# Graph attention over sorted edges: query rows fetched per tile of 128 edges, with one product in place of three

## The chip, the cores and the metric

The kernel runs on one core of a Trainium2 chip. The metric is the device time of one execution in microseconds. The engines are named as in the profile: PE (TensorE, matrix products), PEld (its weight loads), DVE (VectorE), ACT (ScalarE), POOL (GpSimd) and SP (SyncE, which here only starts DMAs and reads the addresses for them).

## The reference

One layer of relational graph attention with a residual and two layer norms. There are 3125 nodes with 128 features, 100,000 edges sorted by destination, 5 edge types (relations) and 8 heads of 16 features. For each relation `r`:

```
q = einsum('eh,khd->ekd', x[dst], W_Q[r]); k, v = the same with x[src], W_K[r], W_V[r]
logits = (q * k).sum(-1) / 4 + attn_bias[r]            # only edges of type r
exp_l  = exp(logits - segment_max(logits, dst)[dst])
attn   = exp_l / (segment_sum(exp_l, dst)[dst] + 1e-12)
out   += segment_sum(attn[:, :, None] * v, dst)
```

Then `out @ out_proj_w.T + out_proj_b`, the residual `x` and a layer norm, the residual again and a second layer norm. An edge needs the query row of its destination and type, and the key and value rows of its source and type.

## The kernel before

**Head.** Nodes come in 25 blocks of 128. For each block the key and value rows of every node and relation are computed (`table`) and stored to DRAM in `kv_d`, one row of 256 float32 for each pair of node and relation. The query rows of a block are split into three bf16 parts whose sum is the float32 row (the value, the remainder, and the remainder of that) and stored in `q_d`, 3 x 128 bf16 for each pair of node and relation; the head does so for the first four blocks. Other jobs prepare, for each edge, the index of its source row, a key that tells its destination and type apart within its group, masks, and `first5`, the row of `q_d` at which a group's window begins. Some sums test that the destinations are sorted and dense enough; if not, a general path runs, which is not executed here.

**Main loop.** Edges come in groups of 512, a group is 4 tiles of 128 edges, and a step has 3 groups, thus 12 tiles (the last two steps have 2 groups). There are 66 steps. Schedule and order are written by hand: each engine runs its instructions in the order of the program, so the order of the calls in the loop (L1003 to L1075) is the order of work. Step k holds work of several steps:

- `gather(k+3)` (L603, POOL): 12 indirect DMAs, one for each tile, bring the key and value rows of 128 edges into one of 6 buffers. Step k+3 takes the buffer that `weigh` has emptied (L817).
- `queries` (L622, PE), for the block due: 3 relations in one step, 2 in the next. The three parts are made by ACT (L627, L636) and DVE (L631, L640).
- `exped(k-2)`: 8 passes on PE bring the exponentials back to the edges (`ex`, L802), ACT copies them (L811). `lanes_turned(k-1)` turns logits (L752), ACT copies (L771).
- `products(k)` (L702, DVE): key rows times the query rows `qe`.
- `spread_q(k+1, [0, 1])` (L688, PE), and later in the step `spread_q(k+1, [2])`: the query row of each edge. `hot` says for each edge which of the 125 rows of the group's window (25 nodes by 5 relations) is its own; the products of `hot` with the three parts add up in PSUM. That is 3 products for each tile, 36 in a step: 24 behind `products`, 12 ahead of the second `sums`.
- `norm(k-3)` (L857 to L861, DVE), the third query part (L640, DVE) and, when a block's rows are complete, `store_q` (L644, SP). Then `relations(k-3)` (`nodes`, L874, PE) and `by_node` (L879, ACT), for which ACT reads a group's first node into a register (L589), one read for each group.
- `weigh(k-2)` (L817, DVE): value rows times exponentials, then `sums` (L845, L841, PE), three times in a step, over the matrices that `places` (L825, L828, ACT) makes.
- `logits(k)` (L722, L711, L728, DVE), `pass_on` (L743, ACT), `turn_next(k-1)` (L752, PE), `spot(k+2)` (`hot`, L675, DVE), `shares(k-1)`: scans (L777, L780) and L787 on DVE, the exponential on ACT (L795).
- `take(k)` on SP: `fetch(k+3)` loads the keys broadcast to 128 partitions (`kt`, L653) and, for each group, reads the row number (L589) and loads 128 rows of 768 bytes (`qw`, L660); then the masks of step k+1 (L667) and, where due, the store of a result block (L945). `kt` has 2 buffers, `qw` 3, `hot` 2.

The blocks that are done are projected, added and normed between (L886 to L937). The lines at which the change touches the loop:

```
products(k)
spread_q(k + 1, [0, 1])
...
third_part(q, c0)
if c0:
    store_q(q)
...
spread_q(k + 1, [2])
if k + 2 < NST:
    spot(k + 2)
...
take(k)
```

Of the kernel before, what the change touches and what calls it, by code (L numbers as in the profile page):

```python
# [50 lines left out]
WR = WN * R  # L51
RH = 3
LANES = R * HEADS
L3 = G3 * LANES
# [70 lines left out]
def windowed_path(  # L125
# [22 lines left out]
    first = keep("first", [1, NGR], I32)  # L148
    first5 = keep("first5", [1, NGR], I32)
    oT = keep("oT", [P, N + WN])  # L150
# [23 lines left out]
    nc.vector.memset(xn[:, NT - 1, :], 0.0)  # L174
    fr = load.tile([1, NGR], I32, name="fr")
    wn = load.tile([2 * R * HEADS, H * HD], F32, name="wn")
# [12 lines left out]
    with nc.allow_non_contiguous_dma(reason="one element of each group"):  # L189
        nc.sync.dma_start(  # L190
            fr[:, : NGR - 1], dst[: (NGR - 1) * GE].rearrange("(o g i) -> o g i", o=1, i=GE)[:, :, 0]
        )
        nc.sync.dma_start(
            fr[:, NGR - 1 : NGR],
            dst[(NGR - 1) * GE : (NGR - 1) * GE + 1].rearrange("(o g) -> o g", o=1),
        )
# [70 lines left out]
    nc.vector.memset(ones, 1.0)  # L267
    vio = keep("vio", [P, 6])
    nc.vector.memset(vio, 0.0)
# [64 lines left out]

    def spills():
# [9 lines left out]
        )  # L345

    gather_heads = keep("gather_heads", [P, G3, HEADS])
# [30 lines left out]
    kvrow = load.tile([HG, 2, GE], F32, name="kvrow")  # L378
    keyr = load.tile([HG, 2, GE], F32, name="keyr")
    typr = load.tile([HG, 2, GE], F32, name="typr")  # L380

    def keys_a():
# [85 lines left out]
    def sorted_ends():  # L468
# [14 lines left out]
        nc.vector.tensor_reduce(vio[0:1, 5:6], lrf[:, 1, :], AX.X, ALU.add)  # L483

    def checks():
        vp = pps.tile([P, 6], F32, name="vp", tag="tr", bufs=2)
        nc.tensor.matmul(vp, ones, vio, start=True, stop=True)
        nc.vector.tensor_reduce(vio[:, 0:1], vp, AX.X, ALU.add)
        nc.vector.tensor_scalar_add(n_bad_i, vio[0:1, 0:1], -float(PADS))

# [40 lines left out]


    first_q = 4
    tps, xts, prs = [], [], []
    for b in range(first_q):
# [5 lines left out]
        for c0, c1 in ((0, RH), (RH, R)):  # L541
# [11 lines left out]
            )  # L553
        nc.sync.dma_start(
            q_d[b * P * R : (b + 1) * P * R, :].rearrange("(p r) c -> p (r c)", r=R),
            q3.rearrange("p r s h -> p (r s h)"),
        )

    sorted_rows()
    short_rows()  # L560
    sorted_ends()
    checks()
    nc.scalar.dma_start(beta_t, beta.partition_broadcast(P))
# [23 lines left out]

    def window(g, table, engine):
        return nc.values_load(  # L589
            table[0:1, g : g + 1],  # L590
            engines=[engine],
            min_val=0,
            max_val=(N - 1) * (R if table is first5 else 1),
            skip_runtime_bounds_check_because="destinations are nodes",
        )

    SPE, ACTE = mybir.EngineType.SP, mybir.EngineType.Activation
# [44 lines left out]
    def store_q(b):  # L642
        live.pop(("xT", b))
        nc.sync.dma_start(  # L644
            q_d[b * P * R : (b + 1) * P * R, :].rearrange("(p r) c -> p (r c)", r=R),
            live.pop(("q3", b)).rearrange("p r s h -> p (r s h)"),
        )

    def fetch(k):
        gs = groups(k)  # L650
        n = len(gs)
        kt = flow.tile([P, G3, GE], BF16, name="kt", bufs=2)
        nc.sync.dma_start(  # L653
            kt[:, :n].rearrange("w g e -> w (g e)"),
            key_d[gs[0] : gs[0] + n].rearrange("g e -> (g e)").partition_broadcast(P),
        )
        qw = flow.tile([P, G3, 3, H], BF16, name="qw", bufs=3)
        for i, g in enumerate(gs):
            f = window(g, first5, SPE)
            nc.sync.dma_start(qw[:, i].rearrange("w s h -> w (s h)"), q_d[bass.ds(f, P), :])  # L660
        live["kt", k], live["qw", k] = kt, qw
# [10 lines left out]
    def spot(k):  # L672
        n = len(groups(k))
        hot = flow.tile([WR, G3, GE], BF16, name="hot", bufs=2)
        nc.vector.tensor_scalar(  # L675
            hot[:, :n], live.pop(("kt", k))[:WR, :n], row_of[:WR], None, op0=ALU.is_equal
        )
        live["hot", k] = hot

    def spread_q(k, which=range(G3)):  # L680
        hot, qw, n = live["hot", k], live["qw", k], len(groups(k))
        if which[0] == 0:
            live["qe", k] = ps.tile([P, T * G3, H], F32, name="qe")
        qe = live["qe", k]
        for i in which:
            for t in range(T if i < n else 0):
                for s in range(3):
                    nc.tensor.matmul(  # L688
                        qe[:, t * n + i, :], hot[:, i, t * P : (t + 1) * P], qw[:WR, i, s, :],
                        start=(s == 0), stop=(s == 2),  # L690
                    )
        if which[-1] == G3 - 1:
            del live["hot", k], live["qw", k]

# [306 lines left out]
    for k in range(NST - 1):  # L1001
# [28 lines left out]
        products(k)  # L1030
        spread_q(k + 1, [0, 1])
        if q is not None:
# [21 lines left out]
        if new:  # L1054
            turn_next(k - 1)
        spread_q(k + 1, [2])
        if k + 2 < NST:
# [583 lines left out]
```

## Time and profile before

| | us |
|---|---|
| median of the runs (3) | 1592.48 |
| lowest and highest | 1590.37 and 1599.27 |
| the profiled execution | 1604.74 |
| its span, first to last instruction | 1602.9 |

| engine | busy us | share of the span |
|---|---|---|
| PE | 1026.0 | 64% |
| PEld | 776.9 | 48% |
| DVE | 887.8 | 55% |
| POOL | 765.3 | 48% |
| ACT | 637.9 | 40% |

The granted clock of PE is 0.689 on average. The first gather starts at 79.9 us and the last at about 1508; in between lie the steps of the main loop, most of them 20 to 24 us long. The DMA engines moved 193.33 MB in 99,495 packets, 18,923 of them under 512 bytes. A line of the table of groups reads: source line, engine, operation, output and inputs, count, then busy us and mean ns of one, then the engine's idle time ahead of it and what ended most of it. "remote" and "another core or an unknown queue" there stand for a wait whose releaser the profile could not name. A line of a timeline reads: start, us, engine, line, operation, output and inputs, count, and in brackets the idle time ahead.

### The profile page before, as it was taken

How to read it: one execution, taken by the hardware profiler on the slowest of the kernel's cores; microseconds unless marked ns; L12 is line 12 of the kernel's file. 1: busy time of each engine (PE TensorE's matmuls, PEld its weight loads, DVE VectorE, ACT ScalarE, POOL GpSimd, SP SyncE). 2: the span in 40 equal slices, each digit the busy share in tenths (PEclk: the TensorE clock that was granted, in tenths of full speed). 3: DMA queues.
4: the chain of work that ended last, by engine and by line, in shares of the span. 5: the costliest groups of instructions: out<-in, count | busy, mean ns of one | idle time of the engine just before them, and what ended most of it. 6: DMA issues, size and time to landing. Idle time of an engine off the chain costs nothing.

```text
span 1602.9 us, 18517 instructions
## 1 busy us (share of the span) xinstructions
PE 1026.0 (64%) x6087; PEld 776.9 (48%) x6087; DVE 887.8 (55%) x1288; ACT 637.9 (40%) x1700; POOL 765.3 (48%) x850
## 2 busy tenths in 40 slices
PE   8930367766657656766657665666556756667985
PEld 4420345544546544554445554455444544455764
DVE  5630455655546555655556655565645655555873
ACT  3410134443434434443434443444434444444662
POOL 2077255555454555455455555555545545455300
PEclk9955667676576677666677666777677766676766
DMA  7655243453443343453444343353344343444300
GB/s 245 265 179 143 87 134 97 123 144 103 119 133 102 106 124 101 118 147 105 117 133 115 101 130 104 110 155 111 106 123 132 97 136 105 120 136 121 80 7 8
DMA packets 99495, 193.33 MB, mean 121 GB/s; under 512 B 18923, under 2 KB 58878, under 8 KB 99270
## 3 DMA queue, kind: packets, MB, share of 16 engines
q0 software_dynamic: 37728, 102.55, 23.9%
q1 hardware_dynamic: 60530, 88.20, 18.0%
q10 hardware_dynamic: 1132, 1.31, 0.3%
q8 instruction: 50, 0.82, 0.2%
q14 instruction: 55, 0.45, 0.1%
HBM read 161.59 MB, written 30.40 MB: 120 GB/s over the span
## 4 chain that ended last, share of the span: by engine, by line
another core or an unknown queue 26%; DVE 26%; PE 22%; ACT 13%; issue 9%; DMA 2%; POOL 1%; DVEq 0%; ACTq 0%
PE both L845 7%; DVE lt L780 4%; DVE lt L777 4%; ACT at L825 4%; PE pr L366 3%; DVE wv L817 3%; PE nodes L874 3%; PE qe L688 3%; DVE lg L722 3%; DVE prod L702 2%; ACT at L828 2%; DMA floor<-in_L_gnn_attn_bias 2%; PE both L841 2%; ACT ls L795 1%
## 5 line engine op out<-in xcount | busy, mean ns | idle before, releaser
L603 POOL DMA_INDIRECT kv<-kv_d,idx x782 | 755.2, 966 | 740.3 <-DVE wv L817 452.6
L688 PE MATMUL qe<-qw,hot 125*128 125x128 bf16 x2352 | 263.3, 277 | 323.9 <-issue 224.4
L688 PEld LDWEIGHTS <-hot 125*128 125x128 bf16 x2352 | 204.0, 127 | 363.9 <-issue 270.5
L845 PE MATMUL both<-wv,at 128*125 128x136 f32 x1568 | 366.3, 375 | 17.6 <-ACT oT L879 10.8
L845 PEld LDWEIGHTS both<-wv,at 128*125 128x125 f32 x1568 | 283.5, 251 | 90.0 <-issue 63.8
L825 ACT ACTIVATE at<-row_at,nkey 128x125 f32<-128x125 f32 x784 | 247.4, 388 | 0.8
L631 DVE TENSOR_TENSOR prq<-prq,q 128x384 f32<-128x384 f32 (+1 forms) x42 | 21.0, 500 | 320.0 <-ACT q L627 320.0
L874 PE MATMUL nodes<-rsum,o 125*128 125x25 f32 x392 | 91.9, 378 | 142.9 <-DVE q L640 136.1
L874 PEld LDWEIGHTS nodes<-rsum,o 125*128 125x128 f32 x392 | 85.6, 315 | 158.2 <-DVE q L640 149.8
L702 DVE TENSOR_TENSOR prod<-kv,qe 128x1536 f32<-128x1536 f32 (+1 forms) x66 | 114.5, 1735 | 65.1 <-remote 59.3
L811 ACT COPY wv<-ex 128x96 f32<-128x96 f32 (+1 forms) x66 | 15.6, 236 | 311.6 <-remote 286.5
L828 ACT ACTIVATE at<-at 128x500 f32<-128x500 f32 x196 | 121.5, 620 | 6.2
L817 DVE TENSOR_TENSOR wv<-kv,ex 128x1536 f32<-128x1536 f32 (+1 forms) x66 | 114.1, 1728 | 10.5 <-ACT wv L811 10.5
L777 DVE TENSOR_TENSOR_SCAN lt<-mk,lt 120x640 f32<-120x640 bf16 (+1 forms) x66 | 98.6, 1493 | 34.5 <-issue 19.7
L722 DVE TENSOR_REDUCE lg<-prod 128x96 f32<-128x1536 f32 (+1 forms) x66 | 115.2, 1745 | 2.3
L780 DVE TENSOR_TENSOR_SCAN lt<-mk,lt 120x640 f32<-120x640 bf16 (+1 forms) x66 | 98.7, 1495 | 2.3
L906 DVE TENSOR_TENSOR h<-pj,xn 128x128 f32<-128x128 f32 (+1 forms) x25 | 7.3, 291 | 158.1 <-remote 140.4
L841 PE MATMUL both<-wv,over 128*5 128x136 f32 x390 | 94.8, 333 | 0.0
L795 ACT ACTIVATE ls<-ls 120x512 f32<-120x512 f32 (+1 forms) x66 | 41.6, 630 | 127.0 <-DVE ls L787 49.2
L752 PE MATMUL lt<-ident,lx 128*120 128x128 f32 (+2 forms) x396 | 84.0, 309 | 4.8 <-DVE lx L711 2.0
L802 PEld LDWEIGHTS ex<-gather_heads,ls 120*128 120x128 f32 (+1 forms) x528 | 75.3, 213 | 20.4 <-issue 10.3
L743 ACT COPY lx<-lx 64x40 f32<-64x40 f32 x65 | 14.4, 222 | 162.5 <-DVE lx L728 153.1
(150 smaller groups left out, 971.4 us busy)
## 6 DMA issues: line engine op xcount, KB each, us to landing
kt<-key_d SPq DMA_DIRECT2D x64, 384.0 KB
qw<-q_d SPq DMA_DIRECT2D x196, 96.0 KB
kv_d<-kvs SPq DMA_DIRECT2D x24, 640.0 KB
kv<-kv_d,idx POOLq DMA_INDIRECT x782
q_d<-q SPq DMA_DIRECT2D x25, 480.0 KB
mk<-msk_d SPq DMA_DIRECT2D x64, 150.2 KB
out<-z SPq DMA_DIRECT2D x24, 64.0 KB
xn<-in_x SPq DMA_DIRECT2D x2, 448.0 KB
```

The costliest lines, as they stand in the source:

```text
L603: nc.gpsimd.indirect_dma_start(out=kv[:, t * n + i, :], out_offset=None, in_=kv_d[:, :], in_offset=bass.IndirectOffsetOnAxis(ap=idx[:, t, ...
L688: nc.tensor.matmul(qe[:, t * n + i, :], hot[:, i, t * P : (t + 1) * P], qw[:WR, i, s, :], start=(s == 0), stop=(s == 2),)
L702: nc.vector.tensor_tensor(prod[:, :n], kv[:, :n, :H], qe[:, :n], op=ALU.mult)
L722: nc.vector.tensor_reduce(lg, heads(live.pop(("prod", k))[:, : T * n]), AX.X, ALU.add)
L777: nc.vector.tensor_tensor_scan(lt, mk[:n, :WIDE], lt, -BIG, op0=ALU.add, op1=ALU.max)
L780: nc.vector.tensor_tensor_scan(lt[:, ::-1], mk[:n, WIDE:0:-1], lt[:, ::-1], -BIG, op0=ALU.add, op1=ALU.max)
L817: nc.vector.tensor_tensor(heads(wv[:, :n, :H]), heads(kv[:, :n, H:]), ex[:, :, :, None].to_broadcast([P, n, HEADS, HD]), op=ALU.mult,)
L825: nc.scalar.activation(at[:, t, :], row_at[:, :WR], AF.Abs, bias=nkey[:, t, g : g + 1], scale=1.0)
L828: nc.scalar.activation(at, at, AF.Relu, bias=1.0, scale=-1.0)
L841: nc.tensor.matmul(pp[:R], over[:, g, :], live["wv", last][:, t * len(groups(last)) + j, :], start=False, stop=False,)
L845: nc.tensor.matmul(pp[:WR], at[:, t, :], wv[:, t * n + i, :], start=(t == 0), stop=(t == T - 1))
L874: nc.tensor.matmul(nodes[:, i], o5[:, i], rsum[:WR], start=True, stop=True)
```

## The change

Each tile of 128 edges gets a window of its own: 8 nodes by 5 relations are 40 rows of 3 parts. In `q_d` each part is now a row of its own (256 bytes), so that a window is 120 rows that follow each other. `qw` holds the 120 rows of each of the 12 tiles, one load for each tile: 12 loads of 120 x 256 bytes in a step in place of 3 loads of 128 x 768. `hot` has 120 partitions, three for each pair of node and relation, and the three parts add up inside one product: 12 products in a step in place of 36, all of them behind `products`. The keys count from the first node of the tile instead of the group; `row_in` is a partition's number divided by 3. The row numbers of a group's four tiles are read together, by one register load on SP for each group; ACT reads the three first nodes of a step in one. `store_q` is moved behind `take`, thus behind the fetches of the step on SP. In the head the first destination of each tile is loaded (781 elements in place of 195, plus the last), and two more sums test that no tile spans more than 8 nodes.

Over the whole run the instructions of `qe` fall from 2352 to 784 on PE; on SP the loads of `qw` rise from 196 to 784.

```diff
+QN = 8
+QR = QN * R
+NTILE = -(-E // P)
...
-    q_d = dram.tile([NP * R, 3 * H], BF16, name="q_d")
+    q_d = dram.tile([NP * R * 3, H], BF16, name="q_d")
...
         nc.sync.dma_start(
-            fr[:, : NGR - 1], dst[: (NGR - 1) * GE].rearrange("(o g i) -> o g i", o=1, i=GE)[:, :, 0]
+            fr[:, : NTILE - 1],
+            dst[: (NTILE - 1) * P].rearrange("(o g i) -> o g i", o=1, i=P)[:, :, 0],
         )
...
-        nc.vector.tensor_copy(frf, fr)
-        nc.vector.tensor_copy(first, frf)
-        nc.vector.tensor_scalar_mul(first5, frf, float(R))
+        nc.vector.tensor_copy(frf, fr[:, ::T])
+        nc.vector.tensor_copy(first, fr[:, ::T])
+        nc.vector.tensor_scalar_mul(first15, fr, float(R * 3))
...
     def lanes():
+        third = load.tile([P, 2], I32, name="third")
+        nc.vector.tensor_scalar_mul(third[:, 0:1], row_of, 171.0)
+        nc.vector.tensor_scalar(
+            third[:, 1:2], third[:, 0:1], 9, None, op0=ALU.arith_shift_right
+        )
+        nc.vector.tensor_copy(row_in, third[:, 1:2])
...
+        nc.vector.tensor_copy(near, keyr[:, :, ::P])
...
-        nc.vector.tensor_copy(keyb, keyr)
+        nc.vector.tensor_tensor(
+            keyb.rearrange("g s (t i) -> g (s t) i", i=P),
+            keyr.rearrange("g s (t i) -> g (s t) i", i=P),
+            near.rearrange("g s t -> g (s t)")[:, :, None].to_broadcast([HG, 2 * T, P]),
+            op=ALU.subtract,
+        )
...
+    def short_tiles():
+        spans = load.tile([HG, 2, T], F32, name="spans")
+        nc.vector.tensor_tensor(
+            spans, dst_r[:, :, P - 1 :: P], dst_r[:, :, ::P], op=ALU.subtract
+        )
...
+    def store_rows(b, q3):
+        nc.sync.dma_start(
+            q_d[b * P * R * 3 : (b + 1) * P * R * 3, :].rearrange("(p c) h -> p (c h)", c=3 * R),
+            q3.rearrange("p r s h -> p (r s h)"),
+        )
...
-    def window(g, table, engine):
-        return nc.values_load(
-            table[0:1, g : g + 1],
+    def starts(table, a, b, engine):
+        _, at = nc.values_load_multi_w_load_instructions(
+            table[0:1, a:b],
             engines=[engine],
...
     def fetch(k):
...
-        kt = flow.tile([P, G3, GE], BF16, name="kt", bufs=2)
+        kt = flow.tile([3 * QR, G3, GE], BF16, name="kt", bufs=2)
...
-        qw = flow.tile([P, G3, 3, H], BF16, name="qw", bufs=3)
+        qw = flow.tile([3 * QR, T * G3, H], BF16, name="qw", bufs=3)
         for i, g in enumerate(gs):
-            f = window(g, first5, SPE)
-            nc.sync.dma_start(qw[:, i].rearrange("w s h -> w (s h)"), q_d[bass.ds(f, P), :])
+            for t, f in enumerate(starts(first15, g * T, (g + 1) * T, SPE)):
+                nc.sync.dma_start(qw[:, t * n + i, :], q_d[bass.ds(f, 3 * QR), :])
...
-        hot = flow.tile([WR, G3, GE], BF16, name="hot", bufs=2)
+        hot = flow.tile([3 * QR, G3, GE], BF16, name="hot", bufs=2)
         nc.vector.tensor_scalar(
-            hot[:, :n], live.pop(("kt", k))[:WR, :n], row_of[:WR], None, op0=ALU.is_equal
+            hot[:, :n], live.pop(("kt", k))[:, :n], row_in[: 3 * QR], None, op0=ALU.is_equal
         )
...
-    def spread_q(k, which=range(G3)):
-        hot, qw, n = live["hot", k], live["qw", k], len(groups(k))
...
-                for s in range(3):
-                    nc.tensor.matmul(
-                        qe[:, t * n + i, :], hot[:, i, t * P : (t + 1) * P], qw[:WR, i, s, :],
-                        start=(s == 0), stop=(s == 2),
-                    )
+    def spread_q(k):
+        hot, qw, n = live.pop(("hot", k)), live.pop(("qw", k)), len(groups(k))
+        live["qe", k] = qe = ps.tile([P, T * G3, H], F32, name="qe")
+        for i in range(n):
+            for t in range(T):
+                nc.tensor.matmul(
+                    qe[:, t * n + i, :], hot[:, i, t * P : (t + 1) * P], qw[:, t * n + i, :],
+                    start=True, stop=True,
+                )
...
-        for i, g in enumerate(groups(k)):
-            f = window(g, first, ACTE)
+        for i, f in enumerate(starts(first, G0[k], G0[k + 1], ACTE)):
             nc.scalar.copy(oT[:, bass.ds(f, WN)], live["nodes", k][:, i])
...
         products(k)
-        spread_q(k + 1, [0, 1])
+        spread_q(k + 1)
...
             third_part(q, c0)
-            if c0:
-                store_q(q)
...
-        spread_q(k + 1, [2])
         if k + 2 < NST:
             spot(k + 2)
...
         take(k)
+        if c0:
+            store_q(q)
```

More of the change, by code (lines that the diff above doesn't have):

```diff
@@ L174, in windowed_path @@
     nc.vector.memset(xn[:, NT - 1, :], 0.0)
-    fr = load.tile([1, NGR], I32, name="fr")
+    fr = load.tile([1, NGR * T], I32, name="fr")
+    nc.vector.memset(fr[:, NTILE:], 0)
     wn = load.tile([2 * R * HEADS, H * HD], F32, name="wn")
@@ L379, in windowed_path @@
     keyr = load.tile([HG, 2, GE], F32, name="keyr")
+    near = load.tile([HG, 2, T], F32, name="near")
     typr = load.tile([HG, 2, GE], F32, name="typr")
@@ L483, in sorted_ends @@
         nc.vector.tensor_reduce(vio[0:1, 5:6], lrf[:, 1, :], AX.X, ALU.add)
+    def short_tiles():
[3 more added lines that the diff above has]
+        )
+        nc.vector.tensor_scalar(
+            spans, spans, float(QN - 1), None, op0=ALU.is_gt, op1=ALU.add,
+            accum_out=vio[:HG, 6:7],
+        )
+        last = load.tile([1, 1], F32, name="last")
+        nc.vector.tensor_tensor(
+            last, lr[:, NGR - 1 :], fr[:, NTILE - 1 : NTILE], op=ALU.subtract
+        )
+        nc.vector.tensor_scalar(
+            vio[0:1, 7:8], last, float(QN - 1), None, op0=ALU.is_gt
+        )
     def checks():
-        vp = pps.tile([P, 6], F32, name="vp", tag="tr", bufs=2)
+        vp = pps.tile([P, 8], F32, name="vp", tag="tr", bufs=2)
         nc.tensor.matmul(vp, ones, vio, start=True, stop=True)
         nc.vector.tensor_reduce(vio[:, 0:1], vp, AX.X, ALU.add)
-        nc.vector.tensor_scalar_add(n_bad_i, vio[0:1, 0:1], -float(PADS))
+        nc.vector.tensor_scalar_add(n_bad_i, vio[0:1, 0:1], -float(PADS + 1))
     typ_ep = {}
@@ L553, in windowed_path @@
             )
[L554 to L557 removed]
+        store_rows(b, q3)
     sorted_rows()
@@ L561, in windowed_path @@
     sorted_ends()
+    short_tiles()
     checks()
@@ L643, in store_q @@
         live.pop(("xT", b))
[L644 to L647, printed above, removed]
+        store_rows(b, live.pop(("q3", b)))
     def fetch(k):
@@ L673, in spot @@
         n = len(groups(k))
-        hot = flow.tile([WR, G3, GE], BF16, name="hot", bufs=2)
+        hot = flow.tile([3 * QR, G3, GE], BF16, name="hot", bufs=2)
         nc.vector.tensor_scalar(
-            hot[:, :n], live.pop(("kt", k))[:WR, :n], row_of[:WR], None, op0=ALU.is_equal
+            hot[:, :n], live.pop(("kt", k))[:, :n], row_in[: 3 * QR], None, op0=ALU.is_equal
         )
         live["hot", k] = hot
-    def spread_q(k, which=range(G3)):
-        hot, qw, n = live["hot", k], live["qw", k], len(groups(k))
[L682 to L686, printed above, removed]
-                for s in range(3):
-                    nc.tensor.matmul(
-                        qe[:, t * n + i, :], hot[:, i, t * P : (t + 1) * P], qw[:WR, i, s, :],
-                        start=(s == 0), stop=(s == 2),
-                    )
-        if which[-1] == G3 - 1:
-            del live["hot", k], live["qw", k]
+    def spread_q(k):
[6 more added lines that the diff above has]
+                    start=True, stop=True,
+                )
     def heads(a):
```

15 lines of the change are left out of this document (9 added, 6 removed).

## The prediction

> **What bounds the kernel now.** I read the table of the costliest groups first, then the waits, then the timelines of TensorE (PE), GpSimd (POOL), ScalarE (ACT) and VectorE (DVE) over one step, 1241 to 1270 us. The groups say which lines are large and what ended the idle time before them:
>
> ```profile
> L603 POOL DMA_INDIRECT kv<-kv_d,idx x782 | 755.2, 966 | 740.3 <-DVE wv L817 452.6
> L688 PE MATMUL qe<-qw,hot 125*128 125x128 bf16 x2352 | 263.3, 277 | 323.9 <-issue 224.4
> L811 ACT COPY wv<-ex 128x96 f32<-128x96 f32 (+1 forms) x66 | 15.6, 236 | 311.6 <-remote 286.5
> ```
>
> No engine is full. POOL is the one with a regular rhythm: the 12 gathers of a step follow each other, 0.95 us and 0.30 us of gap each, and then POOL waits for the weighing on DVE (L817), which gives a buffer back. ACT's copy of the exponentials (L811) waits 286.5 us, 48 times, for something the profile calls remote. The timelines show what that is:
>
> ```profile
> 1246.76 0.95 POOL L603 DMA_INDIRECT kv<-kv_d,idx  x1 [5.17 <-DVE wv L817]
> ...
> 1260.76 0.95 POOL L603 DMA_INDIRECT kv<-kv_d,idx  x1 [0.30 <-issue]
> 1269.06 0.94 POOL L603 DMA_INDIRECT kv<-kv_d,idx  x1 [7.35 <-DVE wv L817]
> ```
> ```profile
> 1243.66 2.74 PE L688 MATMUL qe<-qw,hot 125*128 125x128 bf16 x24 [6.24 <-DVE prod L702]
> ...
> 1249.21 0.84 PE L688 MATMUL qe<-qw,hot 125*128 125x128 bf16 x12
> 1249.89 0.91 PE L845 MATMUL both<-wv,at 128*125 128x136 f32 x6
> ...
> 1254.04 1.07 PE L802 MATMUL ex<-gather_heads,ls 120*128 120x24 f32 x8
> 1254.95 0.83 PE L752 MATMUL lt<-ident,lx 128*120 128x128 f32 x5
> 1256.61 0.61 PE L688 MATMUL qe<-qw,hot 125*128 125x128 bf16 x8 [0.83 <-issue]
> 1258.19 0.26 PE L688 MATMUL qe<-qw,hot 125*128 125x128 bf16 x1 [0.97 <-issue]
> ```
> ```profile
> 1263.93 0.24 ACT L811 COPY wv<-ex 128x96 f32<-128x96 f32 x1 [8.13 <-remote]
> ```
>
> The matmuls `ex` are recorded as ended at 1255.1, but ACT, which waits for nothing else, gets on at 1263.9. From 1256.6 on PE records only one matmul in some 0.7 us, as if a full queue let one in whenever one leaves. Both end about when the block of 12 gathers does (1246.76 to 1261.71). So I read: some microseconds into a block PE really works slower than its records say, and what is left over is finished shortly after the block. SyncE (SP) does the same where gathers run without a pause, at the start (79.9 to 171 us): three loads of `qw` take 10.5 us there and 1.8 us in the loop.
>
> ```profile
> 106.57 10.50 SPq L660 DMA_DIRECT2D qw<-q_d  x3
> ```
> ```profile
> 1250.94 1.80 SPq L660 DMA_DIRECT2D qw<-q_d  x3
> ```
>
> What slows both is not shown; that it goes with the gathers is.
>
> The period follows. Over the 53 steps in which ACT waits so for `ex`, the block takes 14.95 us, the copy L811 starts 1.85 us after its end (mean), and from L811 to the end of L817 it is 4.65 us (mean; 4.86 in the step shown, 1263.93 to 1268.79). With 0.3 us until POOL starts again that is 21.75 us; the mean of these steps is 21.77. So **gathers, lateness of PE, and the chain ACT, DVE, weigh, one behind the other** make the step.
>
> **The change, part by part.**
>
> *Matmuls.* A full step has 36 `qe` matmuls, 24 behind the products and 12 ahead of the second sums. 12 are left, all behind the products, 784 in all instead of 2352. The timelines give 24 in 1.50 to 2.74 us and 12 in 0.84 to 1.46. PE has about 2.1 us less a step. What of it counts is what PE must do between a block's start and `ex`, since the rest hides behind DVE's products and the gathers. That is the 12 ahead of the second sums, 0.84 to 1.46 us, middle 1.15. The lateness it can shorten is 1.85. So 53 x 1.15 = 61 us off; ends 0 (if the gathers' end releases PE whatever stands in the queue) and 53 x 1.85 = 98 (all the lateness). The 24 that become 12 stand behind `ex` in the order and ahead of `nodes`, which waits for DVE (L640) anyway: I cost them at nothing, and 0.75 to 1.4 us a step is there if that cover goes. Next late, when PE is on time, is the end of the gathers themselves.
>
> *Loads of `qw`.* 784 of 120 rows of 256 B in place of 196 of 128 rows of 768 B, so 588 more instructions that start a DMA, each with one or two register instructions. In the loop 1.80 us for three with three register loads is 0.60 each; a fourth of the register loads remains per DMA, so I take 0.4 us: 12 x 0.4 = 4.8 instead of 1.8, +3 us of SP a step. SP waits 649.1 us for the query parts (L640) and 238.8 for `hot`, 14 us a step, so 3 hide. But in the slow phase an instruction of SP takes 0.7 us or more: 10.50 / 12 = 0.88 at the start. Lower end 0, upper end 12 x 3 x 0.88 = 32 us in a step (the rival below). I take 0, since SP has the faster part of every step.
>
> *Packets.* 94,080 in place of 25,088. The hardware queue's mean is 0.18 x 16 x 1602.9 / 60,530 = 76 ns, of larger packets: upper end 69,000 x 76 ns / 16 = 328 us on each DMA engine, 5.1 a step; lower end 0. DMA's share is 0.56 in the block shown and 0.00 in the 6 us behind it, so I take 0. The Trainium skill (DMA: Bandwidth & Descriptors, Specifications) says that a transfer wants 512 B for line rate and is read, modified and written below that, which speaks against the new rows; by it the sum would lie towards the upper end, and no row here has a 256-byte load to weigh it by.
>
> *Store of a query block.* It moves behind the next fetch on SP. The fetch no longer stands behind SP's wait for L640 (21 times, longest 34.7 us), so `kt`, `qw` and the masks leave earlier; they are used two steps later, so nothing ends sooner. The store now waits for the landing of the loads just ahead of it (2 to 3 us, 21 times), with masks and the next `kt` behind it, in the same idle time of SP: 0, ends -20 and +60.
>
> *ACT, DVE.* ACT reads three starts in one register load instead of three; `hot` has 120 partitions instead of 125, 0.60 us as before: 0.
>
> *Head and start.* The first load of destinations has 781 elements of 4 B instead of 196; its issue took 1.04 us, so about 4 now, +3 us for what stands behind it. Eight small DVE operations of 0.25 to 0.35 us lie among others: 0 to +3. In the start 36 loads instead of 9 meet the slow SP, but DVE's first product waits 59.3 us to 178.7 as it is and 24 of 36 slow matmuls go: 0, ends -20 and +25.
>
> **Sum.** Span 1602.9, 1.8 around it, 1604.7 in all. -61 + 3 = -58: 1547. The median shown is 12.3 below the profiled execution: **1535 us**. With the ends for PE (0 to 98) and the start, the forecast's own range is 1475 to 1584.
>
> **The rivals.** About 0.5% (8 us) is what a measurement of this kernel can tell from no change.
>
> *The gathers release PE* (no change, 1584 to 1600): lateness is tied to the last gather, and PE's work does not matter. For it: the copy L811 starts 0.6 to 2.5 us after the block in nearly every step, with queries or without. Against: PE's queue is drained then and its length is work. Nothing saved and the head's 3 us: 1604.7 + 3 - 12.3 = 1595. The granted clock is 0.80 in the block shown and 0.50 in the 6 us behind it; with gaps it could be 0.5 longer, which takes back what is saved. That PE goes back to half rate after an idle window is in the Trainium skill (TensorE: Matmul & The Clock Gate, Part 1); the trace's 0.50 behind the block agrees. 10%.
>
> *PE is the real bound* (1400 to 1475): all 24 matmuls count, as PE's backlog is carried into the next block. 2.1 us x 62 = 130, up to 2.8 x 62 = 174: 1420 to 1465. For: the trickle lasts to the gathers' end. Against: the last steps, without gathers and with all 36, take 13 to 14.7 us. 15%.
>
> *The gathers alone bound* (below 1400): `ex` is done inside the block, POOL never waits, 62 x (21.7 - 15.1) = 409 off 1595: about 1185. Against: with gathers that never stop, PE is slow all the time, as at the start, where 36 matmuls took from 109 to 178. 5%.
>
> *SP becomes the bound* (slower): a fetch is 1 `kt`, 12 loads with two register instructions each, 3 register loads and a mask, some 41 instructions. They fit if most run in the 9 us or so of a step in which SP is fast, at 0.2 to 0.3 us each: 8 to 12 us; the 12 us slow ones take 12 / 0.7 = 17 more. That is close. If the fetch falls mainly into the block, it takes 41 x 0.7 = 29 us; between, 24 us, 2.3 more than the step: +143 with the 3 of the head, 1740. It decides from a fetch of over 21.7 us. For: the start shows it at 0.88 us an instruction, and the small packets add to it. Against: 14 us of waiting in a step. 30%.
>
> A tile over more than its 8 nodes would send the kernel into its general path; with 32 edges a node on average 128 sorted edges touch about 5 nodes, and I give that nothing.
>
> **Chances.** Forecast 40%, PE 15%, gathers 5%, no change 10%, slower 30%. Faster 0.60, same 0.10, slower 0.30. The range takes 1400 to 1700: it leaves out the 5% below and a good third of the slower cases, where they go beyond 1700.
>
> **What would show it.** Right: L688 with 784, its wait for issue far below 224 us; the wait of L811 for remote shorter, and L811 less than 1.85 us behind a block's end; period about 20.6. SP's queue still waits for L640 or `hot`. Wrong: a wait of PE's `qe` or of DVE's `hot` for `qw` or `kt`; L811 as late as before (then the gathers release it); POOL without pauses.

## The result, and the profile after

| | before | after |
|---|---|---|
| median of the runs, us | 1592.76 (4 runs) | 1569.91 (4 runs, 1568.09 to 1573.21) |
| span of the profiled execution, us | 1602.9 | 1571.4 |
| granted clock of PE, mean | 0.689 | 0.617 |

The ratio is 0.9853, 95% interval 0.9819 to 0.9886: faster by 1.5%, where 3.6% was forecast. The time lies within the range of the prediction; of the 57 us that were forecast, 23 came.

The groups of the kernel after, in the columns of the prediction's (the numbers of the lines have moved: L603 is L644 now, L688 L723, L811 L844, L817 L850):

```profile
L644 POOL DMA_INDIRECT kv<-kv_d,idx x782 | 755.0, 966 | 705.8 <-DVE wv L850 414.8
...
L844 ACT COPY wv<-ex 128x96 f32<-128x96 f32 (+1 forms) x66 | 15.7, 238 | 418.7 <-remote 334.6
L723 PE MATMUL qe<-qw,hot 120*128 120x128 bf16 x784 | 77.3, 251 | 104.5 <-issue 44.1
```

Two thirds of the products are gone, and their wait for issue with them (224.4 to 44.1 us). But the wait of ACT's copy of the exponentials has not shrunk; it has grown from 286.5 to 334.6 us. One step of the kernel after, on POOL (start, us, engine, line), then on PE, then on ACT:

```profile
1243.70 0.94 POOL L644 DMA_INDIRECT kv<-kv_d,idx  x1 [7.54 <-DVE wv L850]
...
1257.68 0.95 POOL L644 DMA_INDIRECT kv<-kv_d,idx  x1 [0.30 <-issue]
1265.58 0.94 POOL L644 DMA_INDIRECT kv<-kv_d,idx  x1 [6.96 <-DVE wv L850]
```
```profile
1246.78 1.72 PE L878 MATMUL both<-wv,at 128*125 128x136 f32 x6
1248.43 0.62 PE L874 MATMUL both<-wv,over 128*5 128x136 f32 x2
1248.98 2.07 PE L878 MATMUL both<-wv,at 128*125 128x136 f32 x8
...
1252.07 0.97 PE L835 MATMUL ex<-gather_heads,ls 120*128 120x24 f32 x8
1252.88 0.83 PE L785 MATMUL lt<-ident,lx 128*120 128x128 f32 x5
1253.64 0.84 PE L723 MATMUL qe<-qw,hot 120*128 120x128 bf16 x12
```
```profile
1260.83 0.24 ACT L844 COPY wv<-ex 128x96 f32<-128x96 f32 x1 [7.66 <-remote]
```

`ex` is recorded as done at 1253.0, the last products behind it at 1254.5 with no trickle of single products any more, and yet ACT gets on only at 1260.83, 2.2 us after the block of gathers (1243.70 to 1258.63). In the kernel before it was 2.2 us in the step shown too. That L811 would be as late as before was one of the prediction's own signs of being wrong. The six sums at 1246.78 take 1.72 us; before they took 0.91, behind 12 products.

Where the 31.5 us of span come from, by the timelines: up to the end of the first weighing +14.2 (201.4 to 215.6 us); the next 58 steps -0.84 each (22.14 to 21.30 from weighing to weighing), -48.8; the rest +3.1. A step is the block of gathers (14.95 us in both), the lateness of the copy behind its end, the chain from the copy to the end of the weighing, and 0.27 us. In the mean over the first 54 of these steps:

| kernel | lateness | chain | sum of the two |
|---|---|---|---|
| before | 2.17 | 4.85 | 7.02 |
| after | 2.19 | 3.98 | 6.17 |

So lateness, on which the prediction's 61 us rested, has not moved at all; the chain, which was to stay, is shorter. (The prediction had 1.85 and 4.65 over 53 steps. Leaving out the five longest steps, of 25.6 to 27.3 us, gives 1.86 and 4.62: the prediction's means are close to those of the kernel without its long steps.) And the start costs what was not counted. SP's first loads of `qw`, in the kernel before 10.50 us for three:

```profile
107.67 0.34 SPq L691 DMA_DIRECT2D kt<-key_d  x1
110.70 47.61 SPq L698 DMA_DIRECT2D qw<-q_d  x12
159.00 0.70 SPq L691 DMA_DIRECT2D kt<-key_d  x1
```

### The profile page after: what moved, and what is told of

Its sections match the earlier page's. It is cut to its first block, busy times and chain, and to the rows that moved or that the text cites. A ratio compares the mean times of both kernels' runs of the same rounds, so it can differ in the third digit from the quotient of the medians.

```text
span 1571.4 us, 17061 instructions
## 1 busy us (share of the span) xinstructions
PE 1001.0 (64%) x4519; PEld 738.8 (47%) x4519; DVE 892.1 (57%) x1298; ACT 637.4 (41%) x1700; POOL 765.1 (49%) x850
## 3 DMA queue, kind: packets, MB, share of 16 engines
q1 hardware_dynamic: 138134, 91.45, 20.4%
## 5 line engine op out<-in xcount | busy, mean ns | idle before, releaser
L644 POOL DMA_INDIRECT kv<-kv_d,idx x782 | 755.0, 966 | 705.8 <-DVE wv L850 414.8
L878 PE MATMUL both<-wv,at 128*125 128x136 f32 x1568 | 464.9, 454 | 57.2 <-DVE wv L850 45.8
L878 PEld LDWEIGHTS both<-wv,at 128*125 128x125 f32 x1568 | 359.3, 313 | 159.9 <-issue 88.4
L844 ACT COPY wv<-ex 128x96 f32<-128x96 f32 (+1 forms) x66 | 15.7, 238 | 418.7 <-remote 334.6
L723 PE MATMUL qe<-qw,hot 120*128 120x128 bf16 x784 | 77.3, 251 | 104.5 <-issue 44.1
L850 DVE TENSOR_TENSOR wv<-kv,ex 128x1536 f32<-128x1536 f32 (+1 forms) x66 | 114.2, 1731 | 48.0 <-ACT wv L844 48.0
L874 PE MATMUL both<-wv,over 128*5 128x136 f32 x390 | 116.1, 398 | 0.0
L723 PEld LDWEIGHTS <-hot 120*128 120x128 bf16 x784 | 57.7, 113 | 112.0 <-issue 104.7
L835 PEld LDWEIGHTS ex<-gather_heads,ls 120*128 120x128 f32 (+1 forms) x528 | 88.0, 242 | 18.7 <-ACT ls L828 8.9
L785 PE MATMUL lt<-ident,lx 128*120 128x128 f32 (+2 forms) x396 | 91.4, 332 | 2.9 <-ACT at L861 1.2
L713 DVE TENSOR_SCALAR hot<-kt,row_in 120x1536 bf16<-120x1536 bf16 (+1 forms) x66 | 39.7, 601 | 84.5 <-DMA kt<-key_d 84.5
L835 PE MATMUL ex<-gather_heads,ls 120*128 120x24 f32 (+1 forms) x528 | 81.5, 297 | 8.3 <-ACT ls L828 7.7
```

What stands on the lines that cost most here:

```text
L644: nc.gpsimd.indirect_dma_start(out=kv[:, t * n + i, :], out_offset=None, in_=kv_d[:, :], in_offset=bass.IndirectOffsetOnAxis(ap=idx[:, t, ...
L723: nc.tensor.matmul(qe[:, t * n + i, :], hot[:, i, t * P : (t + 1) * P], qw[:, t * n + i, :], start=True, stop=True,)
L835: nc.tensor.matmul(ex[:, t * n : (t + 1) * n], ls[: n * LANES, t * P : (t + 1) * P], gather_heads[: n * LANES, :n], start=True, stop=True,)
L850: nc.vector.tensor_tensor(heads(wv[:, :n, :H]), heads(kv[:, :n, H:]), ex[:, :, :, None].to_broadcast([P, n, HEADS, HD]), op=ALU.mult,)
L874: nc.tensor.matmul(pp[:R], over[:, g, :], live["wv", last][:, t * len(groups(last)) + j, :], start=False, stop=False,)
L878: nc.tensor.matmul(pp[:WR], at[:, t, :], wv[:, t * n + i, :], start=(t == 0), stop=(t == T - 1))
```

## Theories, and the chips

Theories put to the test: **A** (A1, A2), PE's saved products, all of them or the 12 ahead of the second sums; **B**, the place of the store; **C**, an unbroken run of gathers makes PE and SP slow (the "slow phase"), against **D**, the exponentials wait for the last gather however it is spaced; later **E**, fewer products lower PE's granted clock, against **F** (the store) and **G** (the 12 loads).

The experiments ran in six groups, each on a chip of its own beside the kernel before. This decides what is seen. In the first result, and on two of the six chips that the experiments got, the kernel before takes 1591 to 1597 us. On the other four the same kernel takes 1133 to 1135 us: POOL gathers without a pause, SP shows no stretch of an even 0.7 us an instruction, the slow phase is absent. Each chip was used once, so whether the phase belongs to the chip or to the occasion is not shown. SP's first loads in the changed kernel on such a chip (run e15):

```profile
108.22 0.34 SPq L691 DMA_DIRECT2D kt<-key_d  x1
109.42 7.49 SPq L698 DMA_DIRECT2D qw<-q_d  x12
116.97 0.40 SPq L691 DMA_DIRECT2D kt<-key_d  x1
```

The same 12 loads with the same gathers beside them: 7.49 us here, 47.61 there. All ratios below are to the kernel before on the same chip.

| run | ratio (95%) with the slow phase | without it |
|---|---|---|
| the changed kernel: first result, e5; e15 | 0.985 (0.982 to 0.989), 0.988 (0.983 to 0.993) | 1.028 (1.024 to 1.033) |
| store alone: e8; e1 | 0.981 (0.977 to 0.985) | 1.002 (1.001 to 1.004) |
| changed, store put back: e2 | | 1.027 (1.024 to 1.030) |
| changed, products twice: e6 | 0.985 (0.980 to 0.990) | |
| changed, products thrice: e3, e11, e16, e17 | | 1.000, 1.002, 1.002, 1.004 (each to within 0.003) |
| before, all 36 behind: e7 | 0.955 (0.950 to 0.960) | |
| changed, 12 at the old place: e9 | 0.994 (0.991 to 0.997) | |
| before, 36 behind and store: e12 | | 0.999 (0.997 to 1.002) |
| before, 36 behind, loads split: e13, e18 | | 1.000 (0.997 to 1.003), 1.002 (1.000 to 1.003) |
| changed, pause in the gathers: e10; e4 | 0.895 (0.890 to 0.900) | 1.142 (1.139 to 1.146) |
| before, both moves and pause: e14 | | 1.136 (1.133 to 1.140) |

## The experiments with the slow phase

**The store alone** (e8, and e1 on a chip without the phase).

```diff
             third_part(q, c0)
-            if c0:
-                store_q(q)
...
         take(k)
+        if c0:
+            store_q(q)
```

> The kernel before with the store of a query block moved behind the step's fetches, and nothing else. Theory A (the changed kernel gained its time by the shorter chain behind the exponentials, through PE's saved products): moving the store alone does next to nothing, ratio to the kernel before 0.99 to 1.00. Theory B (the gain is the store's: the kernel before has 5 steps of 25.5 to 27.2 us, the changed one none over 23.0): those five steps lose some 5 us each, 25 us in all, ratio 0.984, and the copy of the exponentials keeps its 4.7 us to the end of the weighing.

> The kernel before with only the store moved, run before where the slow phase was absent (1.002). Where it is present, Theory B: the steps of 25.5 us and more go, ratio 0.98 to 0.99. Theory A2: 0.995 to 1.005.

Without the phase nothing (1.002). With it 0.981: Theory B, and more than the whole change. The five steps of over 25 us are gone, which is most of it, some 25 us; the mean step falls from 22.14 to 21.56. SP's wait for the query parts (total, times, longest; the kernel before, then e8):

```profile
SPq L644 <- DVE q L640: 649.1, 21, 34.7
```
```profile
SPq L644 <- DVE q L640: 212.6, 21, 11.1
```

In the kernel before this wait bunched the fetches: of the 54 blocks of gathers, 20 had no DMA of SP issued in them, 14 had 3 to 6, and 20 had 7 or more. With the store behind the fetches all 54 have 3 to 6, with the old loads: it is the move of the store that puts loads into every block. Lateness and chain are 2.27 + 4.15 = 6.42 us.

**All 36 products behind DVE's products** (e7), the kernel before with one block moved:

```diff
-        spread_q(k + 1, [0, 1])
+        spread_q(k + 1)
...
-        spread_q(k + 1, [2])
```

> The kernel before with the 12 products that stood ahead of the second sums moved up to the other 24, so that all 36 stand behind the products of DVE. Where the slow phase is present, Theory A2 (those 12 delayed the sums, and with them the norm, past the onset of the slow phase): the copy of the exponentials to the end of the weighing falls from 4.7 to some 3.9 us, the ratio to the kernel before is 0.975 to 0.985. Theory B (the store did it): 1.00. Where the slow phase is absent: 1.00, since the gathers without a pause set the step.

0.955: better than forecast, and three times the gain of the whole change, without a single product saved. A2's number was passed, and only in part by A2's way: in the mean the chain did not fall (5.15), lateness fell to 0.60. It fell below 2 us only in blocks in which SP issues next to nothing. ACT and SP of this kernel around such a block (939.62 to 954.57):

```profile
951.00 0.24 ACT L811 COPY wv<-ex 128x96 f32<-128x96 f32 x1 [1.90 <-PE lt L752]
```
```profile
926.88 0.34 SPq L945 DMA_DIRECT2D out<-z  x1
957.24 0.34 SPq L644 DMA_DIRECT2D q_d<-q  x1
957.62 0.43 SPq L653 DMA_DIRECT2D kt<-key_d  x1
960.11 2.03 SPq L660 DMA_DIRECT2D qw<-q_d  x3
```

From 926.88 to 957.24 SP starts no DMA, and the copy comes 3.6 us ahead of the block's end in place of 2.2 behind it. Sorted by SP's DMAs in the block, lateness + chain are:

| DMAs of SP in the block | before | e7 | after |
|---|---|---|---|
| none | 0.91 + 5.52 (20 blocks) | -2.45 + 7.61 (19) | (0) |
| 3 to 6 | 2.25 + 4.86 (14) | 2.72 + 4.67 (15) | 2.39 + 4.86 (2) |
| 7 or more | 3.39 + 4.18 (20) | 2.28 + 2.99 (19) | 2.18 + 3.95 (52) |

(One block of e7 has 1 and is left out. One of its blocks with 3 to 6 lies in the start and is late by 10.6; without it they have 2.16.) A step pays the sum, and an early copy mostly waits again, in a longer chain. With no DMA in the block the sum falls by 1.3 us. With 7 or more it falls by 2.3: these blocks hold the five long steps, which e7 doesn't have, and the norm on DVE, which in the kernel before stands between the copy and the weighing in all 54 steps, does so in 42 of e7. That last part is A2's.

Where SP loads, lateness is 2.2 to 2.4 us in the changed kernel and in e8, and whether PE has 12 or 24 products to do (e6, below) makes no difference then. That loads in the block make the copy late is a reading of this sorting; which blocks have none also depends on what else the step does, and no run changed the loads alone on a chip with the phase.

**Twelve products at the old place** (e9): the changed kernel with the third group's 4 products, issued three times each, ahead of the second sums, and the other 8 where they were.

```diff
-        spread_q(k + 1)
+        spread_q(k + 1, [0, 1])
...
             turn_next(k - 1)
+        spread_q(k + 1, [2], 3)
```

> The changed kernel with the third group's 4 products issued three times each, thus 12 matmuls, ahead of the second sums where they stood before, and the other 8 behind the products. Where the slow phase is present, Theory A2: the gain goes, 4.5 to 4.9 us from the copy to the end of the weighing, ratio to the kernel before 1.00 to 1.02. Theory B: 0.985 to 0.99 as the changed kernel. Where the slow phase is absent: 1.02 (20 products in place of 12, little more clock).

0.994, between the two: more than half of the change's small gain goes, but through the chain (4.18 in place of 3.98) and 0.07 of lateness. In the changed kernel 40 of 54 steps have the norm between the copy and the weighing, here all 54: with the 12 ahead of them the third sums, and the norm that reads them, slip behind the phase. In the 14 steps that this concerns, which make no query rows, lateness and chain are 4.96 in place of 4.21 us; in the other 40 they are 6.96 and 6.87. Theory A2 has this part right, at 0.27 us a step, not 1.15.

**The changed kernel again, and each product twice** (e5, e6).

```diff
+                for again in range(2):
                     nc.tensor.matmul(
...
```

> The changed kernel itself, beside the kernel before, on whatever chip this call gets. In the runs of the first four experiments the kernel before took 1133 us in place of 1593, POOL's gathers followed each other without a pause and SP's instructions never fell to 0.70 us each, so the slow phase of the first profile was absent. Theory E (the change lowers the clock that PE is granted, 0.79 to 0.67, because PE's products become fewer and not because of the store): where the slow phase is absent, ratio 1.02 to 1.03 at a clock of 0.66, like the version with the store put back. Theory F (the version with the store put back was slow because of the store alone): ratio 0.99 to 1.00 at a clock near 0.79. Where the slow phase is present again: 0.985, as in the first result.

> The changed kernel with each product of the query rows issued twice (24 a step). Theory E: PE has more to do than in the changed kernel and is not slower for it: where the slow phase is absent, the granted clock lies between 0.66 and 0.79 and the ratio to the kernel before between 1.00 and 1.02. Theory F: no difference from the changed kernel. Where the slow phase is present: within 0.5% of the changed kernel.

e5 repeats the first result (0.988). Products twice: 0.985, lateness 2.19, chain 3.98, to the hundredth the changed kernel's. With the phase, what stands behind DVE's products costs nothing, as the prediction said, and A1 falls. The granted clock rose little: 0.626 to 0.641 in its runs, 0.623 to 0.627 in those of e5 on the same chip.

**A pause between the sixth and the seventh gather** (e10, and e4 without the phase): memsets on POOL, 2.7 us together.

```diff
+                if done == 6 and k >= KVB:
+                    for again in range(5):
+                        nc.gpsimd.memset(rest_t, 0.0)
+                done += 1
```

> The changed kernel with a pause of some 1.5 to 3 us on POOL between the sixth and the seventh gather of a step. Theory C (an unbroken run of gathers slows PE and SP from 8 us after its start to its end: in the trace SP's instructions take 0.08 to 0.6 us before that point and 0.70 us from it on): no half reaches 8 us, PE is on time, the copy of the exponentials no longer waits for the end of the block, and a step takes 17 to 19 us in place of 21.2: 1320 to 1450 us, ratio 0.83 to 0.91. Rival D (the exponentials wait for the last gather of the block, however it is spaced): the block ends later by the pause, +1.5 to 3 us a step, ratio 1.04 to 1.10.

> The changed kernel with 2.7 us of pause on POOL between the sixth and the seventh gather of a step; it ran before where the slow phase was absent and took 18 us a step, 1.142. Where the slow phase is present, Theory C (only an unbroken run of over 8 us slows PE and SP): the slow phase goes, the step is POOL's 15.05 + 3.1 = 18.1 us, some 1320 us, ratio 0.83. Rival D (the wait lasts to the last gather however it is spaced): +3 us a step, 1.11.

D falls, and Theory C holds in the main. With the phase the ratio is 0.895, though POOL is given more to do. ACT and POOL of this kernel:

```profile
1002.40 0.24 ACT L850 COPY wv<-ex 128x96 f32<-128x96 f32 x1 [1.04 <-PE ex L841]
1020.31 0.22 ACT L850 COPY wv<-ex 128x96 f32<-128x96 f32 x1
```
```profile
1016.01 0.95 POOL L650 DMA_INDIRECT kv<-kv_d,idx  x1 [0.30 <-issue]
1016.96 2.80 POOL L648 MEMSET rest_t<- 1x512 f32 x5
1019.92 0.95 POOL L650 DMA_INDIRECT kv<-kv_d,idx  x1 [0.16 <-issue]
```

The copy hardly waits for a nameless releaser any more (6.1 us, once, in place of 334.6 us, 47 times): at 1002.40 it waits 1.04 us for `ex` itself, at 1020.31 for nothing. The step is 19.06 us, not the 18.1 of POOL alone, as POOL still waits for the weighing in 18 steps of the loop, 83.5 us in all. SP is not quite free of the phase: 12 loads in the loop still take 11.8 and 10.8 us. (This kernel's profiled execution lies 1.0% above its median of 1432.97.) Without the phase the pause is only 3 us more in a step that POOL bounds: 1.142.

## The experiments without the slow phase

Here the gathers alone bound the kernel before, at about 1134 us. The prediction's third rival had that at 1185 us, as an effect of the change; on these chips it holds already without the change, and the changed kernel is slower.

**The changed kernel, with and without the store's move** (e15, e2: the store put back into the middle of the step, the reverse of the diff above).

> The changed kernel itself once more. Where the slow phase is absent, Theory E: 1.02 to 1.03 at a clock near 0.66, as with the store put back; Theory F (the store): 0.99 to 1.00. Where it is present: 0.985 to 0.988 as measured twice.

> The changed kernel with the store of a query block put back to its old place, in the middle of the step. Theory A: as the changed kernel, ratio to the kernel before 0.985 to 0.99. Theory B: the gain is gone, since the start is 14 us later and only the store made up for it: 1.00 to 1.01, with single steps of 25 us or more again.

1.028 and 1.027: the store makes no difference, F falls. The windows from 400 to 800 us (PE busy, PEld, DVE, ACT, POOL, PEclk, DMA share, GB/s) of the changed kernel and, on the same chip, of the one with its products issued three times (e16):

```profile
400.00:800.00 400.00, 345.70 (x1655) 261.71 (x1654) 322.76 (x445) 235.53 (x631) 303.52 (x317) 0.64 0.70 175
```
```profile
400.00:800.00 400.00, 339.98 (x2429) 271.24 (x2430) 341.65 (x474) 250.06 (x678) 303.26 (x318) 0.83 0.72 180
```

**Products thrice** (e3, e11, e16, e17): as above with `range(3)`, 36 products in a step.

> The changed kernel with each product of the query rows issued three times over (36 a step again, the same value each time), all behind the products of DVE. Theory A1 (PE's amount of work counts): 24 matmuls more a step at 0.06 to 0.11 us put 1.5 to 2.7 us back into a step, ratio to the kernel before 1.03 or more. Theory A2 (only the 12 that stood ahead of the second sums counted, because they delayed the third sums and with them the norm; what stands behind the products is covered): within 0.3% of the changed kernel, ratio 0.985 to 0.99.

> The changed kernel with each product three times, 36 in a step behind the products of DVE; it ran before only where the slow phase was absent. Where it is present, Theory E (fewer products leave PE at a lower granted clock, 0.62 in place of 0.69, so that the sums behind them take longer and the 12 saved are given back): like the kernel before with all 36 behind, the copy of the exponentials starts under 1 us after the block and the ratio is 0.96 to 0.97, that one's 0.955 and 14 us of a later start. Theory G (the 12 loads and their packets give it back): as the changed kernel, 0.985, the copy 2.2 us behind the block.

> The changed kernel with each product three times, which ran twice where the slow phase was absent (1.000 and 1.002 at a clock of 0.79 to 0.80). Where it is present, Theory E: 0.96 to 0.97, the copy of the exponentials under 1 us behind the block. Theory G: 0.985, the copy 2.2 us behind. Where it is absent: 1.00 again, below the changed kernel beside it, although PE has 24 products more in a step.

> The changed kernel with each product three times, so far run only where the slow phase was absent. Where it is present, Theory E (the clock gives the gain back): 0.96 to 0.97, the copy of the exponentials under 1 us behind the block. Theory G (the loads do): 0.985, the copy 2.2 us behind. Where it is absent: 1.00.

Theory E: 1568 products more, all of them superfluous, make the changed kernel faster, 1165.69 to 1135.96 us on one chip. The granted clock is 0.83 in place of 0.64 in that window, so 774 more matmuls take less busy time. One group carries most of it, the sums; over the whole run, e15, then e16 (one line further down):

```profile
L878 PE MATMUL both<-wv,at 128*125 128x136 f32 x1568 | 452.7, 445 | 38.2 <-DVE wv L850 19.4
```
```profile
L879 PE MATMUL both<-wv,at 128*125 128x136 f32 x1568 | 362.0, 369 | 43.7 <-ACT at L862 16.3
```

And the chain that ended last lies mostly on PE where the clock is low. e16, with 36 products, and then e15:

```profile
PE 27%; DVE 27%; POOL 16%; issue 9%; ACT 8%; DMA 5%; SPq 1%; ACTq 0%; DVEq 0%
```
```profile
PE 63%; DVE 15%; ACT 9%; issue 3%; DMA 2%; POOL 1%; SPq 1%; ACTq 0%; DVEq 0%
```

That PE falls to half rate after an idle window is stated by the Trainium skill (TensorE: Matmul & The Clock Gate, Part 1). That the clock follows what PE does agrees; but PE's records show it busy for 345.7 of 400 us at 0.64, and the longest gap in its records of that window is 2.4 us, where e16 has one of 3.6 us at 0.83. So what lowers the clock here is not idleness that the records show, and the measurement decides. Which property of the bf16 products holds it up was not tried.

**The two moves without the new layout, and the loads split** (e12: both diffs on the kernel before; e13 and e18: e7 with each load split by rows).

```diff
-            nc.sync.dma_start(qw[:, i].rearrange("w s h -> w (s h)"), q_d[bass.ds(f, P), :])
+            for j in range(4):
+                nc.sync.dma_start(
+                    qw[j * 32 : (j + 1) * 32, i].rearrange("w s h -> w (s h)"),
+                    q_d[bass.ds(f + j * 32, 32), :],
+                )
```

> The kernel before with all 36 products behind the products of DVE and the store behind the fetches, with its 3 loads of 768-byte rows kept: the changed kernel's two moves without its new layout. Where the slow phase is present: 0.955 and 0.981 together, at most 0.937, at least 0.955 if both shorten the same wait. Where it is absent: 1.00.

> The kernel before with all 36 products behind the products of DVE and each load of query rows split into 4 of 32 rows of 768 bytes, thus 12 loads a step with the same bytes and packets. Theory G: the gain of that kernel, 0.955, falls to 0.98 or above, by more than the start takes (the first weighing ends some 14 us later, 0.009). Theory E: 0.955 to 0.966, the copy 0.6 us behind the block as without the split. Where the slow phase is absent: 1.00 to 1.005.

> The kernel before with all 36 products behind the products of DVE and its loads split into 12 in a step, so far run only where the slow phase was absent (1.000). Where it is present, Theory G: 0.98 or above. Theory E: 0.955 to 0.966, the copy 0.6 us behind the block. Where it is absent: 1.00.

> The kernel before with both moves and the pause of 2.7 us on POOL between the sixth and the seventh gather. Where the slow phase is present: the step is POOL's 18.1 us, 1320 to 1430 us, ratio 0.83 to 0.895, better than the changed kernel with the pause (0.895) by the earlier start and the higher clock. Where it is absent: 1.14.

0.999, 1.000, 1.002: without the phase neither the place of the 12 products nor 12 loads in a step cost anything measurable. e14, both moves with the pause, takes 1.136, POOL's 18 us a step. None of these kernels ran on a chip with the phase, so E against G is not settled there. That the gains of the two moves do not add up has a likely reason in e8: the store's move puts loads into every block, and the blocks without loads are where e7's copy came early. No run with the phase has tested it, or separated the number of loads from their being spread over all blocks, or from the lower clock.

## Why the prediction was wrong

- *What bounds it* was right: gathers, lateness, and the chain, one behind the other; PE and SP are slowed by the gathers (C, by e10). It was not seen that only some chips do this, and the means over 53 steps come close to those without the five long steps.
- **The step that failed** is the term of the matmuls, "53 x 1.15 = 61 us off", with lateness as what it shortens. Lateness went from 2.17 to 2.19: 0. The rival to which 10% was given, that the gathers release PE whatever stands in the queue, was right for the blocks in which SP loads: there lateness is 2.2 to 2.4 us with 12 products behind DVE's (the changed kernel), with 24 (e6) and, but for one block in the start, with 36 (e7). What the 12 products do cost in the changed kernel, by e9, is 0.27 us a step, some 16 us in 58 steps, through the chain. In the kernel before, moving them alone gave 70 us (e7, 1597 to 1528); that this is near 61 is luck, since much of it comes from the long steps and the chain, which the term did not have.
- *The store*, costed at 0 with ends -20 and +60, gives 1.9% alone, 32 us, beyond its own end: it ends the five steps of over 25 us, and with them the chain falls by 0.70 us in the mean. The working had asked only when the loads are used, not what the bunching does to the block in which they fall.
- *The loads*, 12 x 0.4 us and hidden: SP does hide them. They lie in 54 of 54 blocks, where before 20 had none, but by e8 the store's move does that without them. The two moves gain 4.5% and 1.9% alone; together with the new loads 1.5%. In the loop nothing measured charges the new loads with a loss; in the start they cost (next point).
- *The start*, 0 with ends -20 and +25, and +3 for the head: measured +14.2, of which the head is 3.3 (first gather 79.9 to 83.3), as forecast. The first 12 loads take 47.6 us in the slow phase; the first product comes 18 us earlier as hoped, but the second step waits for SP.
- *Packets*: the bound was 5.1 us a step. The hardware queue's share of the DMA engines went from 18.0% to 20.4%, which is 0.204 x 1571.4 - 0.180 x 1602.9 = 32 us on each engine in place of 328. The sentence that the Trainium skill (DMA: Bandwidth & Descriptors, Specifications) has on transfers below 512 B pointed to the upper end. On chips without the phase the 256-byte rows cost next to nothing (thrice, 1.000 to 1.004), but there the gathers set the step and can hide them.
- *SP as the bound* did not happen. The waits that were to show it, of `qe` for `qw` (37.1 us) and of `hot` for `kt` (84.5 us), lie in the start but for 3.1 us between 260 and 1440 us. *The clock* was named under the rival of no change; on chips without the phase it is what decides, and there the forecast's sign is wrong: 1.028.
- *The sum*: with the ends that it names, 0 to 98 for PE and -20 to +25 for the start, the range comes to 1477 to 1620, not 1475 to 1584.

So with the phase 58 us were forecast and 31.5 came. The steps gave -48.8: by e8 some 34 are the store's (0.58 a step), by e9 some 16 the 12 products', through the chain and not through lateness. The start took back 14.2 and the end 3.1.

The version to keep is e7, the kernel before with its 36 products together: 0.955 with the phase, and with further edits 0.999 to 1.002 without it (e12, e13, e18).

## What to carry to other kernels

Take out one part of a change at a time: here either of two moves of a few lines, alone, gained more than the whole rewrite (4.5% and 1.9% against 1.5%), and gains that were measured alone need not add up. Work that is removed from an engine shortens nothing while that engine's results wait for something else; find what the wait ends with before counting instructions. And run the same kernel on more than one chip before a stall is explained, since a stall that makes 29% of the time (1597 against 1134 us) may not be there on the next.

## What the runs showed of the hardware that was not expected

- In the first result and on two of the six chips of the experiments SP and PE become slow while gathers run without a break. In the step shown of the kernel after, SP's instructions take 0.6 us or less until 7 us after the block's start; from 8.5 us on only one, or a pair, ends about every 0.70 us, until some 2 us behind the block's end. A pause of 2.7 us after six gathers lifts most of it (0.895). The kernel before takes 1597 us on such a chip and 1134 on one without. What causes it was not found.
- SP and the results of PE come free about together: in that step the block ends at 1258.63, ACT's copy starts at 1260.83, and the last of SP's 12 loads ends at 1261.14. First this step on SP, then one of e15, where the phase is absent:

```profile
1247.82 13.32 SPq L698 DMA_DIRECT2D qw<-q_d  x12
```
```profile
609.89 7.36 SPq L698 DMA_DIRECT2D qw<-q_d  x12
```

- Without the phase PE's granted clock is 0.665 in the changed kernel, against about 0.80 in the kernel before, and 1568 superfluous bf16 products bring it back to 0.79, with 2.6% of the time (e15, e16).
